# A four-layer graph network: smaller last chunks and two groups' sums a turn in layers 2 and 3, one tile of lanes, gather lists kept or loaded early

## The chip, the cores and the metric

The kernel runs on one core of a Trainium2 chip. A core has five engines with an instruction queue each: PE (matmuls; its weight loads are shown apart, as PEld), DVE (elementwise work, reductions and scans), ACT (activation functions and scaled copies), POOL (here mostly the indirect DMAs, which gather or scatter rows by a list of indices) and SP (plain DMAs). An engine works through its queue in order and waits on semaphores for the others. The metric is the device time of one execution in microseconds; times of ten executions and one profiled execution are given.

## The reference

Four layers act on 6250 nodes with 128 features and 200,000 edges, sorted by their target `dst`. Each layer adds to `x`, from `h = relu(layernorm(x))`. What matters here are layers 2 and 3, both of which weigh edges by a softmax:

```python
# layer 2 (h and edge_weight1 in)
xl = x @ Wl + bl;  xr = x @ Wr + br
m = leaky_relu(xl[src] + xr[dst] + edge_attr @ We, 0.2)
logits = m @ att
ex = exp(logits - segment_max(logits, dst)[dst])
alpha = ex / (segment_sum(ex, dst)[dst] + 1e-16)
out = segment_sum(xl[src] * alpha[:, None], dst)
# x + out, gelu, and a normalisation over the nodes follow

# layer 3 (heads = src, rels = edge_type, tails = dst)
score = sum(e_t * tanh(e_h + e_r), axis=-1)
score_exp = exp(score - max(score))
attn = score_exp / (segment_sum(score_exp, heads)[heads] + 1e-10)
agg = segment_sum(attn[:, None] * e_t, heads)
out = leaky_relu((entity_emb + agg) @ W.T, 0.2)
```

Layer 0 sums `h[src]` over `dst`, layer 1 sums messages made of `(x @ W_in)[dst]` and an edge filter over `src`; dense layers follow in both.

## The kernel before

**Groups.** The edges are cut into 391 groups (`NG`) of 512 (`FE`), that is four tiles (`FT`) of 128 edges, one edge to a partition. A group's targets lie in a window of 64 nodes (`FW`), which begins at a register value (`starts`), so that sums over edges become matmuls against a one-hot matrix. Such a matrix comes from a comparison of `lane`, a tile that holds 0 to 63 in each of four tiles, with `loc`, the edges' targets less the window's start. If the edges are not sorted, or a window is too wide, a general path runs; with these inputs it does not.

**Stages.** Layer 0 gathers rows of `h` by `src` and adds up windows (with the edges' ranks by `src` for layer 1 beside it); layer 1 first makes messages and scatters them in the order of `src` (`messages1`), then reads them back in that order and sums them (`windows1`); `node2` makes the tables `l_tab` and `r_tab`. Layer 2 is `windows2` with `sums2`; `node3` finishes it (`finish2`), and makes `g_tab` and `w_tab`. Layer 3 is `windows3` with `sums3`, and `finish3` writes the output.

**A group in layers 2 and 3** goes through these steps, of which `in_chunks` calls one for one group in each turn:

- `fetch`: four gathers into `m` (POOL, L328, rows of `l_tab` by `src`, or of `g_tab` by `dst`), the window `win` and rows of edge data (SP), and the one-hot matrix `hotT` on DVE (L1196, L1509).
- `near`: four matmuls `pz` (L1204, L1518); in layer 3 a tanh to `z` on ACT (L1520).
- `scores`: DVE makes one score for each edge (L1210 to L1213; L1526).
- `weights`, once for a chunk of 12 groups (`CG`): a running maximum and exponentials in several steps, one step a turn (five `yield`s in layer 2, L1220 to L1279, two in layer 3, L1534 to L1555); its result `ex` goes to `todo`.
- `weighted`: the one-hot `hot` by a comparison with `lane` (DVE, L1291, L1566), times `ex` on ACT (L1293, L1568).
- `sums`: matmuls of `m` by `hot` into `ps` (L1300 and L1301; L1577, and L1578 with a DVE reduction L1574 ahead of it).
- `add`: DVE adds `ps` to `acc` (L1308 and L1311; L1586 and L1587).

A turn fetches group g, weighs one group of `todo`, sums the one weighed a turn ago, does `near` for group g-1 and `scores` for g-2, adds what was summed a turn ago, and takes one step of `weights`. When the last group is fetched, turns go on until `todo` is empty.

**What sets the order.** Except for layer 1's messages, whose order is written out, the framework that builds the program orders each engine's instructions itself: it takes the order of the code as priority and what it reckons to be ready. Buffers come from pools of fixed size: 25 `m` in layer 2 and 27 in layer 3, two `ps`, three `hot`; an instruction that writes a buffer waits for the last reader of the one before.

**Lists.** Layer 0 loads `src` into a tile `src0` in its own pool, which ends with layer 0; layer 2 loads it again (L1162) and layer 3 loads `dst`, in the order of `src`, from `o_tab[1]` (L1475), where layer 1 left it. Layers 0, 1, 2 and 3 each make `lane` with an iota on POOL (L870, L1050, L1168, L1481).

Of the kernel before, what the change touches and what calls it, by code (L numbers as in the profile page):

```python
# [9 lines left out]
F32 = mybir.dt.float32  # L10
I32 = mybir.dt.int32
# [12 lines left out]
P = 128  # L24
# [44 lines left out]
def gnn_kernel(ctx: ExitStack, tc: tile.TileContext, t, out):  # L69
# [108 lines left out]
    bad_b = const.tile([1, 1], I32, name="bad_b")  # L178
    nc.vector.memset(bad_b, 1)

    upto1 = ExitStack()
    pos = upto1.enter_context(tc.tile_pool(name="pos", bufs=1)).tile([P, NG * FT], I32, name="pos")
    upto0 = ExitStack()
    src0 = upto0.enter_context(tc.tile_pool(name="src0", bufs=1)).tile([P, NG * FT], I32, name="src0")
    with tc.tile_pool(name="h", bufs=1) as hp, tc.tile_pool(name="ln", bufs=1) as lp:
        h = hp.tile([P, J, D], F32, name="h")
        norm_relu(lp, h, lambda c: nc.scalar.dma_start(nodes(h_tab)[:, c:c + CJ, :], h[:, c:c + CJ, :]))


        nc.sync.dma_start(first, t["dst_first"].rearrange("(o g) -> o g", o=1))  # L190
        with tc.tile_pool(name="ok", bufs=1) as op, tc.tile_pool(name="ok_ps", bufs=1, space=PSUM) as pp:
            ds_ = op.tile([P, 2, EP // P], I32, name="ds")
            for k in range(2):
                nc.sync.dma_start(ds_[:, k, :], t["dst_pad"][k:k + EP].rearrange("(p n) -> p n", p=P))
            df = op.tile([P, 2, EP // P], F32, name="df")
# [12 lines left out]
            nc.vector.tensor_tensor(fl[:, 1, :], fl[:, 1, :], fl[:, 0, :], op=ALU.subtract)  # L208
            nc.vector.tensor_scalar(fl[:, 1, :], fl[:, 1, :], float(FW) - 0.5, None, op0=ALU.is_gt)
            wide_ = op.tile([1, 1], F32, name="wide_")  # L210
            nc.vector.tensor_reduce(wide_, fl[:, 1, :], axis=AX.X, op=ALU.add)
            pv = pp.tile([1, 1], F32, name="pv")
            nc.tensor.matmul(pv, viol, ones[:, 0:1], start=True, stop=True)
            nc.vector.tensor_tensor(bad, pv, wide_, op=ALU.add)
        nc.sync.dma_start(src0, t["src_f"])


    def load(name, shape, src):
# [631 lines left out]
    def windows0():  # L850

        with ExitStack() as st:
# [3 lines left out]
            with ExitStack() as st:  # L856
# [6 lines left out]
                src = src0  # L863
                rank = ranks(st, src)
                loc = lp.tile([P, NG, FT], F32, name="loc")
                nodes_ = loc.bitcast(I32)
                nc.sync.dma_start(nodes_.rearrange("p g j -> p (g j)"), t["dst_f"])
                nc.vector.tensor_tensor(loc, nodes_, bcast(base, FT), op=ALU.subtract)
                lane = lp.tile([P, FT, FW], F32, name="lane")
                nc.gpsimd.iota(lane, pattern=[[0, FT], [1, FW]], base=0, channel_multiplier=0,  # L870
                               allow_small_or_imprecise_dtypes=True)
# [28 lines left out]
    upto0.close()  # L900


    def messages1():
# [133 lines left out]
    def windows1():  # L1037

        messages1()
        with ExitStack() as st:  # L1040
# [3 lines left out]
            with ExitStack() as st:  # L1044
# [4 lines left out]
                lane = one.tile([P, FT, FW], F32, name="lane")  # L1049
                nc.gpsimd.iota(lane, pattern=[[0, FT], [1, FW]], base=0, channel_multiplier=0,  # L1050
                               allow_small_or_imprecise_dtypes=True)
# [40 lines left out]
        windows1()  # L1092
    with cond.Else():
        zeroed(sums[1])
        phase(edges1, ["f_src", "dst", "w_col", "attr"],
              functions="natural_log_exp_and_others")
        node2(lambda: finish_sums(sums[1], None, w_o1, b_o1, shifted_softplus, w_o2, b_o2))
# [4 lines left out]
    def in_chunks(sp, fetch, near, scores, weights, weighted, sums, add):  # L1102

        sc, ms, todo = None, [], []
        one, two, held = None, None, None
        hot, part = None, None
        g = 0  # L1110
        while g < NG or one or two or held or todo or hot or part:
            new = (g, fetch(g)) if g < NG else None
            new_hot = None
            if todo:
                a, m, i, ex, scale, more = todo.pop(0)
                new_hot = a, weighted(a, m, ex[:, i * FT:(i + 1) * FT], *more), scale
            new_part = (hot[0], sums(hot[0], hot[1]), hot[2]) if hot else None
            new_two = (one[0], near(*one)) if one else None
            if two:
                b, got = two  # L1120
                i = b % CG
                if i == 0:
                    sc, ms = sp.tile([P, CG * FT], F32, name="sc"), []
                ms.append((b, scores(b, got, sc[:, i * FT:(i + 1) * FT])))
            if part:
                add(*part)
            if held:
                try:
                    next(held[0])
                except StopIteration as e:  # L1130
                    ex, scale, *more = e.value
                    todo += [(a, m, a % CG, ex, scale if i == 0 else None, more)
                             for i, (a, m) in enumerate(held[1])]
                    held = None
            if two and (b % CG == CG - 1 or b == NG - 1):
                held = weights(b // CG * CG, len(ms) * FT, sc), ms
                next(held[0])
            one, two, hot, part = new, new_two, new_hot, new_part
            g += 1

    def windows2():
# [9 lines left out]
    def sums2(st, acc):  # L1151
# [6 lines left out]
        pp = st.enter_context(tc.tile_pool(name="ep", bufs=2, space=PSUM))  # L1158
        cp = st.enter_context(tc.tile_pool(name="ec", bufs=2, space=PSUM))
        RW = 2  # L1160
        src = lp.tile([P, NG * FT], I32, name="src")
        nc.sync.dma_start(src, t["src_f"])  # L1162
        loc = lp.tile([P, NG, FT], F32, name="loc")
        nodes_ = loc.bitcast(I32)
        nc.sync.dma_start(nodes_.rearrange("p g j -> p (g j)"), t["dst_f"])
        nc.vector.tensor_tensor(loc, nodes_, bcast(base, FT), op=ALU.subtract)
        lane = lp.tile([P, FT, FW], F32, name="lane")
        nc.gpsimd.iota(lane, pattern=[[0, FT], [1, FW]], base=0, channel_multiplier=0,  # L1168
                       allow_small_or_imprecise_dtypes=True)
# [145 lines left out]
    def node3(finish):  # L1315

        with tc.tile_pool(name="h3", bufs=1) as hp, tc.tile_pool(name="y", bufs=2) as yp, \
                tc.tile_pool(name="y_ps", bufs=2, space=PSUM) as pp, tc.tile_pool(name="ln", bufs=1) as lp:
            finish()
            h = hp.tile([P, J, D], F32, name="h")  # L1320
            rest = hp.tile([FW, D], F32, name="rest")
# [142 lines left out]
    def sums3(st, acc, top):  # L1464
# [15 lines left out]
        lane = lp.tile([P, FT, FW], F32, name="lane")  # L1480
        nc.gpsimd.iota(lane, pattern=[[0, FT], [1, FW]], base=0, channel_multiplier=0,  # L1481
                       allow_small_or_imprecise_dtypes=True)
# [248 lines left out]
```

## Time and profile before

| | us |
|---|---|
| median of ten executions (lowest to highest) | 10489.92 (10475.3 to 10502.91) |
| the profiled execution | 10494.47 |
| its span, first to last instruction | 10492.7 |
| layer 0 | 0 to 2430 |
| layer 1, messages, then sums and `node2` | 2430 to 4950, to 5434 |
| layer 2, then `node3` | 5434 to 7916, to 8028 |
| layer 3, then `finish3` | 8028 to 10447, to the end |
| last gather of layer 2, of layer 3 begins | 7842.84, 10382.1 |

The page gives, over the whole span, PE 6903.5 us busy (66%), DVE 5307.3 (51%), ACT 2292.4 (22%) and POOL 6380.4 (61%). Its second part cuts the span into 40 slices of 262 us; a digit is the busy share in tenths, and PEclk is the clock that was granted to PE, in tenths of full speed. A group of instructions is shown by line, engine and operation, `out<-in`, with its count, then the busy time and the mean in ns, then the idle time ahead of it and what ended it. "issue" is time in which an engine waited for nothing that the profile shows, "remote" or "another core or an unknown queue" a releaser that the profile cannot name. The four-pass float32 matmuls appear as two entries each, so the four matmuls of `near` are "x8". In the instructions in order of time, a line has start, duration, engine, line, operation, and in brackets the idle time before it with its releaser.

### The profile page before, as it was taken

The numbers are of one execution on the slowest core, as the hardware profiler recorded it, in microseconds if no ns is written. First come the engines' busy times: TensorE is split into PE (matmuls) and PEld (weight loads), VectorE is DVE, ScalarE is ACT, GpSimd is POOL, SyncE is SP. The second block draws the span as 40 slices with busy tenths as digits, with TensorE's granted clock in tenths as the row PEclk, the third lists the DMA queues.
The fourth block names the chain that finished last, engine by engine and source line by source line (L and its number), as shares of the span: only waits on it lengthen the run. The fifth ranks groups of instructions, "written<-read, shape, count | busy, mean of one in ns | idle before, by whom it ended". The sixth has DMA issues, their size and how long they took to land.

```text
span 10492.7 us, 122048 instructions
## 1 busy us (share of the span) xinstructions
PE 6903.5 (66%) x31854; PEld 5216.2 (50%) x31854; DVE 5307.3 (51%) x21299; ACT 2292.4 (22%) x6433; POOL 6380.4 (61%) x6281
## 2 busy tenths in 40 slices
PE   4788888855555655555955666666663567777677
PEld 3444444434444444444944454554452466666666
DVE  5455555524444444444765566665664444444445
ACT  0000000003444444443221111111112222222223
POOL 6666666664666666665026777777762566666663
PEclk9755555557777777777986666666665555555555
DMA  2111111113333333333942222222222333333332
GB/s 81 45 47 46 43 43 45 42 46 90 96 98 97 98 97 98 98 98 106 291 150 66 71 72 72 71 73 71 72 65 86 90 96 92 95 93 95 94 94 85
DMA packets 462742, 893.64 MB, mean 85 GB/s; under 512 B 150146, under 2 KB 232501, under 8 KB 461891
## 3 DMA queue, kind: packets, MB, share of 16 engines
q1 hardware_dynamic: 251274, 451.64, 15.1%
q0 software_dynamic: 200192, 412.80, 14.9%
q10 hardware_dynamic: 10556, 21.01, 0.6%
q8 instruction: 281, 4.60, 0.2%
q14 instruction: 439, 3.60, 0.1%
HBM read 750.87 MB, written 133.98 MB: 84 GB/s over the span
## 4 chain that ended last, share of the span: by engine, by line
PE 47%; another core or an unknown queue 21%; DVE 13%; issue 10%; POOL 4%; ACT 3%; DMA 2%; DVEq 0%; SPq 0%; ACTq 0%; POOLq 0%
PE pz L1518 6%; PE ps L1577 5%; PE ps L881 5%; PE pw L973 4%; PE ps L1066 3%; POOL m L328 3%; PE py L975 3%; PE pf L952 3%; PE pq L797 3%; PE ps L1300 3%; PE pz L1204 3%; PE sizes L765 2%; PE pq L798 2%; PE ps L1301 1%
## 5 line engine op out<-in xcount | busy, mean ns | idle before, releaser
L328 POOL DMA_INDIRECT m<-l_tab,src x1564 | 1746.5, 1117 | 662.4 <-issue 409.1
L332 POOL DMA_INDIRECT m_tab<-m,pos x1564 | 1588.2, 1015 | 871.7 <-issue 442.0
L328 POOL DMA_INDIRECT m<-h_tab,src x1564 | 1533.3, 980 | 852.5 <-issue 423.5
L328 POOL DMA_INDIRECT m<-g_tab,dst x1564 | 1506.4, 963 | 847.9 <-issue 411.1
L1518 PE MATMUL pz<-win,hotT 128*128 128x128 f32 x3128 | 848.2, 424 | 360.6 <-issue 282.2
L1577 PE MATMUL ps<-hot,m 128*128 128x64 f32 x3128 | 734.8, 408 | 404.8 <-ACT hot L1568 242.7
L973 PEld LDWEIGHTS pw<-L_gnn_W_f,sp_r 128*128 128x128 f32 x3128 | 496.1, 234 | 960.2 <-issue 918.0
L973 PE MATMUL pw<-L_gnn_W_f,sp_r 128*128 128x128 f32 x3128 | 532.2, 324 | 649.7 <-DVE sp_r L999 463.2
L1577 PEld LDWEIGHTS ps<-hot,m 128*128 128x128 f32 x3128 | 670.1, 313 | 531.2 <-ACT hot L1568 341.8
L1204 PE MATMUL pz<-win,hotT 128*128 128x128 f32 x3128 | 660.6, 369 | 365.8 <-issue 210.6
L1518 PEld LDWEIGHTS pz<-win,hotT 128*128 128x128 f32 x3128 | 712.4, 315 | 371.2 <-issue 316.5
L881 PEld LDWEIGHTS ps<-hot,m 128*128 128x128 f32 x3128 | 731.0, 326 | 299.6 <-issue 111.9
L1204 PEld LDWEIGHTS pz<-win,hotT 128*128 128x128 f32 x3128 | 556.2, 263 | 594.5 <-issue 367.3
L881 PE MATMUL ps<-hot,m 128*128 128x64 f32 x3128 | 722.8, 408 | 192.7 <-DVE acc L883 64.9
L1293 ACT ACTIVATE hot<-hot,ex 128x64 f32<-128x64 f32 x1564 | 415.9, 336 | 1868.1 <-DVE hot L1291 1019.7
L1300 PE MATMUL ps<-hot,m 128*128 128x64 f32 x3128 | 585.0, 347 | 270.5 <-issue 91.2
L983 DVE TENSOR_TENSOR m<-pw,L_gnn_b_f_b 128x512 f32<-128x512 f32 x391 | 267.6, 685 | 961.5 <-remote 660.6
L1300 PEld LDWEIGHTS ps<-hot,m 128*128 128x128 f32 x3128 | 546.7, 262 | 318.9 <-issue 259.9
L975 PE MATMUL py<-win,hotT 128*128 128x128 f32 x3128 | 533.7, 314 | 210.3 <-issue 210.1
L952 PE MATMUL pf<-row_a,w_f1p 128*128 128x512 f32 x782 | 511.2, 728 | 158.6 <-issue 136.1
L1520 ACT ACTIVATE z<-pz 128x512 f32<-128x512 f32 x391 | 232.7, 596 | 1664.2 <-PE pz L1518 887.4
L883 DVE TENSOR_TENSOR acc<-acc,ps 128x64 f32 x391 | 86.7, 222 | 1005.7 <-PE ps L881 456.3
(322 smaller groups left out, 12250.4 us busy)
## 6 DMA issues: line engine op xcount, KB each, us to landing
m<-m_tab SPq DMA_DIRECT2D x391, 262.0 KB
row<-in_dst_row SPq DMA_DIRECT2D x390, 256.0 KB
row<-e_tab SPq DMA_DIRECT2D x390, 256.0 KB
row_w<-in_w_row SPq DMA_DIRECT2D x195, 256.0 KB
m<-h_tab,src POOLq DMA_INDIRECT x1564
m_tab<-m,pos POOLq DMA_INDIRECT x1564
m<-l_tab,src POOLq DMA_INDIRECT x1564
m<-g_tab,dst POOLq DMA_INDIRECT x1564
```

The lines of the kernel that those rows point to most:

```text
L328: nc.gpsimd.indirect_dma_start(out=dst, out_offset=None, in_=table[:], in_offset=bass.IndirectOffsetOnAxis(ap=idx, axis=0))
L332: nc.gpsimd.indirect_dma_start(out=table[:], out_offset=bass.IndirectOffsetOnAxis(ap=idx, axis=0), in_=src, in_offset=None, **kw)
L797: nc.tensor.matmul(pq, pick[:, i:i + 1].to_broadcast([3 * RB, P]), pieces[b], start=True, stop=False)
L881: nc.tensor.matmul(ps, m[:, j, :], hot[:, j, :], start=(j == 0), stop=(j == FT - 1))
L952: nc.tensor.matmul(pf, w_f1p, attrs[g // RW % 3][:, along(g)], start=True, stop=True)
L973: nc.tensor.matmul(pw[:, j, :], sp[:, j * P:(j + 1) * P], w_f2, start=True, stop=True)
L975: nc.tensor.matmul(py[:, j, :], hots[g % 4][:, j * P:(j + 1) * P], wins[g % 8], start=True, stop=True)
L1204: nc.tensor.matmul(pz[:, j, :], hot[:, j * P:(j + 1) * P], win[g % 4], start=True, stop=True)
L1293: nc.scalar.activation(hot[:, j, :], hot[:, j, :], AF.Copy, scale=ex[:, j:j + 1])
L1300: nc.tensor.matmul(ps[:, 0, :], m[:, j, :], hot[:, j, :], start=(j == 0), stop=(j == FT - 1))
L1518: nc.tensor.matmul(pz[:, j, :], hot[:, j * P:(j + 1) * P], win[g % 4], start=True, stop=True)
L1577: nc.tensor.matmul(ps[:, 0, :], m[:, j, :], hot[:, j, :], start=(j == 0), stop=(j == FT - 1))
```

## The change

`lane` and a list `taken` become tiles that live for the whole kernel. `lane` is made once, at the start. `taken` holds `src` from layer 0 through layer 2, so that layer 2 loads nothing; `node3` then loads `o_tab[1]` into it ahead of its own finish, and layer 3 gathers by it. (The general path of layer 1 stores `taken` to `o_tab[1]`; it does not run here.)

In `in_chunks`, chunks end at 12, 24, up to 360, then at 367, 373, 379, 385 and 391: one of seven groups and four of six, in place of two of 12 and one of seven. In turns after the 367th, two groups of `todo` are weighted, and with that summed and added, if two are there. The steps of a turn also come in another order: fetch, add, sums, weighted, near, scores, weights, where before it was fetch, weighted, sums, near, scores, add, weights. All groups are still computed as before.

```diff
+    lane = const.tile([P, FT, FW], F32, name="lane")
+    nc.gpsimd.iota(lane, pattern=[[0, FT], [1, FW]], base=0, channel_multiplier=0,
+                   allow_small_or_imprecise_dtypes=True)
+    taken = const.tile([P, NG * FT], I32, name="taken")
...
-    src0 = upto0.enter_context(tc.tile_pool(name="src0", bufs=1)).tile([P, NG * FT], I32, name="src0")
...
-        nc.sync.dma_start(src0, t["src_f"])
+        nc.sync.dma_start(taken, t["src_f"])
...
+        full = (NG // CG - 2) * CG
+        ends = set(range(CG, full + 1, CG)) | set(range(NG, full + CG // 2 - 1, -(CG // 2)))
+        tail = NG - 2 * CG
         sc, ms, todo = None, [], []
         one, two, held = None, None, None
-        hot, part = None, None
+        hot, part = [], []
         g = 0
         while g < NG or one or two or held or todo or hot or part:
             new = (g, fetch(g)) if g < NG else None
-            new_hot = None
-            if todo:
+            for p in part:
+                add(*p)
+            part = [(a, sums(a, got), scale) for a, got, scale in hot]
+            hot = []
+            for _ in range(2 if g > tail and len(todo) > 1 else min(1, len(todo))):
                 a, m, i, ex, scale, more = todo.pop(0)
-                new_hot = a, weighted(a, m, ex[:, i * FT:(i + 1) * FT], *more), scale
-            new_part = (hot[0], sums(hot[0], hot[1]), hot[2]) if hot else None
+                hot.append((a, weighted(a, m, ex[:, i * FT:(i + 1) * FT], *more), scale))
             new_two = (one[0], near(*one)) if one else None
             if two:
                 b, got = two
-                i = b % CG
-                if i == 0:
-                    sc, ms = sp.tile([P, CG * FT], F32, name="sc"), []
+                if not ms:
+                    sc = sp.tile([P, CG * FT], F32, name="sc")
+                i = len(ms)
                 ms.append((b, scores(b, got, sc[:, i * FT:(i + 1) * FT])))
-            if part:
-                add(*part)
...
-            if two and (b % CG == CG - 1 or b == NG - 1):
-                held = weights(b // CG * CG, len(ms) * FT, sc), ms
+            if two and b + 1 in ends:
+                assert held is None
+                held = weights(ms[0][0], len(ms) * FT, sc), ms
+                ms = []
                 next(held[0])
...
     def sums2(st, acc):
-        src = lp.tile([P, NG * FT], I32, name="src")
-        nc.sync.dma_start(src, t["src_f"])
+        src = taken
-        lane = lp.tile([P, FT, FW], F32, name="lane")
-        nc.gpsimd.iota(lane, ...)
...
     def node3(finish):
+            nc.sync.dma_start(taken, o_tab[1])
             finish()
...
     def sums3(st, acc, top):
-        dst = lp.tile([P, NG * FT], I32, name="dst")
-        nc.sync.dma_start(dst, o_tab[1])
+        dst = taken
-        lane = lp.tile([P, FT, FW], F32, name="lane")
-        nc.gpsimd.iota(lane, ...)
```

More of the change, by code (lines that the diff above doesn't have):

```diff
@@ L179, in gnn_kernel @@
     nc.vector.memset(bad_b, 1)
+    lane = const.tile([P, FT, FW], F32, name="lane")
+    nc.gpsimd.iota(lane, pattern=[[0, FT], [1, FW]], base=0, channel_multiplier=0,
+                   allow_small_or_imprecise_dtypes=True)
+    taken = const.tile([P, NG * FT], I32, name="taken")
     upto1 = ExitStack()
     pos = upto1.enter_context(tc.tile_pool(name="pos", bufs=1)).tile([P, NG * FT], I32, name="pos")
-    upto0 = ExitStack()
-    src0 = upto0.enter_context(tc.tile_pool(name="src0", bufs=1)).tile([P, NG * FT], I32, name="src0")
     with tc.tile_pool(name="h", bufs=1) as hp, tc.tile_pool(name="ln", bufs=1) as lp:
@@ L862, in windows0 @@
                 tp = st.enter_context(tc.tile_pool(name="et", bufs=1, space=PSUM))
-                src = src0
+                src = taken
                 rank = ranks(st, src)
@@ L868, in windows0 @@
                 nc.vector.tensor_tensor(loc, nodes_, bcast(base, FT), op=ALU.subtract)
-                lane = lp.tile([P, FT, FW], F32, name="lane")
-                nc.gpsimd.iota(lane, pattern=[[0, FT], [1, FW]], base=0, channel_multiplier=0,
-                               allow_small_or_imprecise_dtypes=True)
                 own = own_terms(acc, hp, tp)
@@ L898, in gnn_kernel @@
         node1(lambda: finish_sums(sums[0], h_tab, w1_0, b1_0, relu_bias, w2_0, b2_0))
-    upto0.close()
     def messages1():
@@ L1048, in windows1 @@
                 tp = st.enter_context(tc.tile_pool(name="et", bufs=2, space=PSUM))
-                lane = one.tile([P, FT, FW], F32, name="lane")
-                nc.gpsimd.iota(lane, pattern=[[0, FT], [1, FW]], base=0, channel_multiplier=0,
-                               allow_small_or_imprecise_dtypes=True)
                 ids = one.tile([P, NG, FT, IDS], F32, name="ids")
@@ L1094, in gnn_kernel @@
         zeroed(sums[1])
+        nc.sync.dma_start(o_tab[1], taken)
         phase(edges1, ["f_src", "dst", "w_col", "attr"],
@@ L1131, in in_chunks @@
                     ex, scale, *more = e.value
-                    todo += [(a, m, a % CG, ex, scale if i == 0 else None, more)
+                    todo += [(a, m, i, ex, scale if i == 0 else None, more)
                              for i, (a, m) in enumerate(held[1])]
                     held = None
-            if two and (b % CG == CG - 1 or b == NG - 1):
-                held = weights(b // CG * CG, len(ms) * FT, sc), ms
+            if two and b + 1 in ends:
+                assert held is None
+                held = weights(ms[0][0], len(ms) * FT, sc), ms
+                ms = []
                 next(held[0])
-            one, two, hot, part = new, new_two, new_hot, new_part
+            one, two = new, new_two
             g += 1
@@ L1160, in sums2 @@
         RW = 2
-        src = lp.tile([P, NG * FT], I32, name="src")
-        nc.sync.dma_start(src, t["src_f"])
+        src = taken
         loc = lp.tile([P, NG, FT], F32, name="loc")
@@ L1166, in sums2 @@
         nc.vector.tensor_tensor(loc, nodes_, bcast(base, FT), op=ALU.subtract)
-        lane = lp.tile([P, FT, FW], F32, name="lane")
-        nc.gpsimd.iota(lane, pattern=[[0, FT], [1, FW]], base=0, channel_multiplier=0,
-                       allow_small_or_imprecise_dtypes=True)
         node = lp.tile([FW, NG], F32, name="node")
@@ L1479, in sums3 @@
         nc.vector.tensor_tensor(loc, si.rearrange("p (g j) -> p g j", j=FT), bcast(base_b, FT), op=ALU.subtract)
-        lane = lp.tile([P, FT, FW], F32, name="lane")
-        nc.gpsimd.iota(lane, pattern=[[0, FT], [1, FW]], base=0, channel_multiplier=0,
-                       allow_small_or_imprecise_dtypes=True)
         node = lp.tile([P, NG], F32, name="node")
```

## The prediction

> **What bounds the kernel now.** I read the page first, then the chain that ended last, then busy time by stretch, and last the instructions in order of time at the places that the diff touches. The page shows that layers 2 and 3 (slices 21 to 40) are neither idle nor full on any engine, so a share over the whole span decides nothing:
>
> ```profile
> POOL 6666666664666666665026777777762566666663
> PEclk9755555557777777777986666666665555555555
> ...
> L328 POOL DMA_INDIRECT m<-l_tab,src x1564 | 1746.5, 1117 | 662.4 <-issue 409.1
> ```
>
> The stretches tell it better (columns: length, then busy us and count of PE, PEld, DVE, ACT, POOL, then granted PE clock, DMA share, GB/s):
>
> ```profile
> 5650.00:7700.00 2050.00, 1332.48 (x6582) 1009.91 (x6581) 1280.38 (x5793) 370.66 (x1418) 1512.45 (x1346) 0.66 0.27 72
> ...
> 7700.00:7842.00 142.00, 85.90 (x410) 63.56 (x409) 78.21 (x350) 22.64 (x86) 102.84 (x95) 0.64 0.26 69
> 7864.90:7915.90 51.00, 50.40 (x188) 32.99 (x186) 21.68 (x97) 17.91 (x69) 0.00 (x0) 0.50 0.02 3
> 10240.00:10382.00 142.00, 102.55 (x436) 92.91 (x437) 68.19 (x325) 36.88 (x124) 90.71 (x95) 0.52 0.35 95
> 10412.40:10447.20 34.80, 33.44 (x156) 32.60 (x156) 22.74 (x76) 15.30 (x59) 0.00 (x0) 0.52 0.01 1
> ```
>
> Row 1: in layer 2's body POOL is busy 1512 of 2050 us, and POOL's waits there hold 347.5 us of "issue" (0.30 before every gather), together 91%: **the gathers set the pace**, 6.1 us a turn (391 groups of four gathers from 5450 to 7843), and PE idles 35%. Rows 3 and 5: once the last gather and the last score are done, PE alone works, 50.40 of 51.00 us and 33.44 of 34.80 us. These are the **drains**. The chain shows one, a group's sums after another at 1.90 + 0.94 = 2.84 us:
>
> ```profile
> 7906.78 1.90 PE ps L1300 x8
> 7908.68 0.94 PE ps L1301 x2
> 7909.62 1.90 PE ps L1300 x8
> 7911.52 0.94 PE ps L1301 x2
> 7912.46 1.91 PE ps L1300 x8
> 7914.39 3.67 DMA hs<-k_tab
> ```
>
> Row 4: in layer 3 PE is busy 102.55 of 142 us with gathers still running; POOL waits for PE there (146.5 us for pz L1518, 84.0 for ps L1578 from 8250 to 10240), so layer 3 is paced by PE and its round trip over ACT.
>
> The starts of both layers, POOL's instructions in order of time:
>
> ```profile
> 5434.54 0.35 POOL L1168 IOTA lane<- 128x256 f32 x1 [484.04 <-DMA r_tab<-r]
> 5439.37 0.98 POOL L328 DMA_INDIRECT m<-l_tab,src  x1 [4.49 <-DMA src<-in_src_f]
> ...
> 8028.36 0.35 POOL L1481 IOTA lane<- 128x256 f32 x1 [184.58 <-DMA w_tab<-w]
> 8033.39 0.97 POOL L328 DMA_INDIRECT m<-g_tab,dst  x1 [4.68 <-DMA dst<-o_tab]
> ```
>
> At 5434.54 POOL may run, but the first gather waits until 5439.37 for the list `src`; likewise at 8028.36 for `dst`.
>
> **The change part by part.** The working is made against the profiled execution: 10494.47 us, a span of 10492.7 and 1.77 around it; it lies 4.55 above the median of the ten, 10489.92.
>
> *Lists kept (layer 2) or loaded early (layer 3).* Layer 2's load goes, layer 3's is issued in `node3` ahead of its finish. SP has nothing from the last gather (7842.84) to 7910.72 but that, the same load took some 5 us at 8028.20, and the first that queues behind it is a small store that nobody awaits; cost 0. Without that cover it would push back the `d_tab` store of 7916.04 by 5 us. The first gather moves to where POOL was free (the iota, 0.35 us, goes too): 5439.37 - 5434.54 = 4.8 and 8033.39 - 8028.36 = 5.0. From there to 5590 and to 8179 the chain is mostly waits on an unseen queue in steps of about 22 us per four groups, which is the gathers' landing, so an earlier first gather should move all of it. What is late next is DVE's memsets and loads (first compare at 5453.31 and 8052.22), but those feed the first groups only. I take -4.8 and -5.0. Bounds: 0 each if DVE's preparation gates; +3.3 for layer 2, since one early gather took 8.16 us (at 5441.92, under DVE's 10.62 us memset), and a second of that length would cost 8.16 - 4.8.
>
> *Lanes in one tile.* Four iotas of 0.35 us become one. Those of layers 0 and 1 (34.9, 4937.9) stand before a first compare at 53.9 and 4955.2: 0. Those of layers 2 and 3 lie inside the list's wait, counted above.
>
> *Chunks and two sums a turn.* Writing both loops out turn by turn: 412 turns become 403 in layer 2 and 409 become 400 in layer 3; sums left after the last score fall from 18 to 12 and from 15 to 6; 8 groups' sums move ahead of the last fetch in layer 2, and 9 ahead of the last score in layer 3. Each layer has two chunks more (35 for 33).
>
> Layer 2 drain: six sums fewer, 6 x 2.84 = 17.0. New on the path: the last chunk's weights. In the trace they take 7865.56 to 7878.57, 13.0 us; six other sums (17.0) now lie beside them, so they are hidden, but the first `hot` after them is not: 0.41 on DVE and 0.35 on ACT, about 1. Drain -16. Without that cover it would be -17 + 13. The turns 390 to 392, the last with a score, have no sums, so the 22.1 us from the last gather to the last score shrink: -2 (0 to -5). POOL's five long waits between 7690 and 7845 (3.82, 1.38, 2.75, 1.82, 2.11) are for `m` buffers; live groups fall from 21 of 25 to 12 to 16, so they can go: a third, -4 (0 to -11.9). What pays is 8 x 2.84 = 22.7 us of PE inside 142 - 85.9 = 56 us of PE idle. Taken: **-22**. Bounds: -33 with every wait gone; +6.7 if the moved sums lengthen the turns by all they cost (22.7 - 16).
>
> Layer 3 drain: nine sums fewer at 1.71 + 0.43 = 2.14 are 19.2; the weights (max, matmul, max, matmul, exp) now stand alone with about 4. So -15. But here PE paces the turns: the nine cost 9 x (1.97 + 0.53) = 22.5 us of 39.5 us idle, of which about 1.0 a turn (pz ends, ACT's z 0.60, first `hot` 0.35, then sums) comes once in each of 23 turns however many sums it has. 39.5 - 23 = 16.5 is open, 6 is paid. Taken: **-9**; bounds -15 and +7.5 (22.5 - 15).
>
> The added chunks: layer 2's weights are some 5.4 us on DVE and 2.4 on PE, twice, beside gathers: 0, or +11 without them.
>
> *`add` first in the turn.* The `add` of the turn before now stands ahead of sums, weighted and scores. It frees a `ps` buffer (there are two) earlier. The row for it:
>
> ```profile
> PE ps L1300 <- DVE acc L1311: 69.8, 66, 3.0
> ```
>
> 69.8 us is the most that can be had, and PE is not the bound there: POOL leaves 9% open, 69.8 x 0.09 = 6. Taken -6, bounds -69.8 and 0 for layer 2, since 0.81 us of `add` (0.40 + 0.20 + 0.21) ahead of `hot` fits into PE's 2.4 idle us a turn. In layer 3 the order already stands so in time (acc at 10366.01, hotT 10366.22, hot 10367.09): 0.
>
> On the clock: the drain of layer 2 is 99% busy and was granted 0.50; between 7857 and 7863 the same sums took 1.08 + 0.59 = 1.67 us at a higher clock. The Trainium skill (TensorE: Matmul & The Clock Gate, Part 1: The HAM clock gate) says that half rate is the default and that about 3.4 us of sustained activity releases it. By that the six sums would be worth 6 x 1.67 = 10 instead of 17. The row speaks against it for these matmuls, and the row is used above.
>
> Sum: -4.8 - 5.0 - 22 - 9 + 0 - 6 = **-46.8**: 10447.7 for the profiled execution, 10443.1 when it is taken from the median, as all times below are.
>
> **Rivals.** *The work is hidden nowhere:* moved sums lengthen the turns by their full price. For it: layer 3's PE pace, the ACT round trip. Against: PE's 56 us idle in layer 2. -9.8 + 6.7 + 7.5 = +4.4: 10494. (That the lists bring nothing, since DVE gates, adds 9.8 to any case.)
>
> *The new order pays in full:* PE's 69.8 us all come back. For it: the long chain of DVE work behind which `add` stood. Against: POOL's 91%. -46.8 - 63.8 = -110.6: 10379.
>
> *Slower, by the order in layer 3:* `both` (L1574) waits for ACT's `hot` 113 times, 123.3 us in all; it now stands ahead of the `hot` compare L1566 on DVE. Should each wait pass on to L1566, ACT and PE's sums, layer 3 pays 123.3: -46.8 + 123.3 = +76.5, 10566. It decides from 46.8 + 21 = 67.8 us on, over half of these waits. Against: L1566 at 10367.09 is consumed only a turn later.
>
> **How the numbers follow.** 0.2% (21 us) is about what a measurement of this kernel tells from no change. Forecast 0.55, its own range -25 to -65 (starts by half, -5, with layer 2's drain of -16 and layer 3's at -4; or -9.8 - 33 - 15 - 6, all bounds of gain but the order's): 10425 to 10465. Hidden nowhere 0.17, the "same" case. New order 0.15. Slower 0.13. Faster is 0.55 + 0.15 = 0.70. The range reaches from the new order's 10379, rounded to 10380, to 10500, past the hidden case; what it leaves out is the slower case and a little at the low end.
>
> **What would show it.** Right: the first gathers of layers 2 and 3 directly behind the landing of `r_tab` and `w_tab`; 12 and 6 groups' sums after the last score; the drains about 35 and 20 us long; the body of each layer as long as before to within 10 us. Wrong: turns of 8 us from group 368 on in layer 3; POOL waiting for `m` in the tail; a body of layer 2 or 3 changed by more than 20 us, which only the order can do. If DVE gates the starts, the first scores stand where they stood.

## The result, and the profile after

The changed kernel takes **10525.33 us** (median; 10514.13 to 10534.62) against 10489.92: the ratio is 1.0035, with a 95% interval of 1.0026 to 1.0043. It is slower, where 10443 was forecast and faster was given 0.70. Its profiled execution took 10505.74 us (span 10503.9), some 20 us less than its median, so its trace holds only 11 of the 35 us.

From the page of the changed kernel, the lines that answer to those of before:

```profile
POOL 6666666664666666665025767777753566666663
PEclk9655555557777777777976666666655655555556
...
L331 POOL DMA_INDIRECT m<-l_tab,taken x1564 | 1664.2, 1064 | 1208.8 <-issue 887.6
```

Layer 2's gathers became shorter (1064 ns each for 1117), and POOL waits longer instead. Its first gathers, in order of time:

```profile
5417.51 0.98 POOL L331 DMA_INDIRECT m<-l_tab,taken  x1 [482.87 <-issue]
...
8027.39 0.94 POOL L331 DMA_INDIRECT m<-g_tab,taken  x1 [219.78 <-issue]
```

Layer 2's first gather starts 21.9 us earlier, not 4.8: with iota and list gone, it doesn't wait for `r_tab` either. Last the tails, as busy time by stretch with the prediction's columns; first of the kernel before, from the 341st group's score to the last score of layer 2, and from there to the last `add`; then the same two stretches of the changed kernel, and its two of layer 3:

```profile
7572.90:7862.22 289.32, 197.67 (x963) 148.38 (x962) 186.79 (x847) 54.25 (x209) 200.84 (x180) 0.66 0.26 69
7862.22:7915.68 53.46, 51.97 (x196) 34.29 (x196) 24.14 (x111) 18.68 (x72) 0.00 (x0) 0.52 0.02 2
```

```profile
7542.01:7877.06 335.05, 242.47 (x1049) 183.57 (x1049) 202.18 (x924) 62.17 (x241) 185.59 (x177) 0.58 0.23 61
7877.06:7914.93 37.87, 35.35 (x134) 22.89 (x134) 16.41 (x79) 11.63 (x46) 0.00 (x0) 0.50 0.02 2
10150.48:10439.60 289.12, 200.53 (x995) 183.94 (x993) 151.00 (x728) 90.80 (x303) 154.92 (x161) 0.59 0.31 83
10439.60:10460.15 20.55, 17.99 (x81) 16.91 (x80) 11.36 (x45) 6.57 (x27) 0.00 (x0) 0.50 0.00 0
```

The drain is 15.6 us shorter, but the stretch ahead of it 45.7 us longer: layer 2's tail, which was to give 22 us, costs 30. The whole ledger follows, from the instructions in order of time. Marks: a, the first gather of the layer; b, c, d, the scores of groups 25, 341 and 391; e, the last `add`. The right-hand columns are for the experiments below (`before_again`, `after_third` and `fix_pool`).

| us | before | changed | quick chip: before | changed | list on POOL |
|---|---|---|---|---|---|
| a of layer 2 stands at | 5439.4 | 5417.5 | 4665.7 | 4654.9 | 4647.7 |
| layer 2, a to b | 208.2 | 220.1 | 143.8 | 144.3 | 143.7 |
| b to c, the body | 1925.3 | 1904.4 | 1817.6 | 1700.1 | 1698.4 |
| c to d | 289.3 | 335.0 | 286.0 | 327.5 | 276.5 |
| d to e, the drain | 53.5 | 37.9 | 54.0 | 37.9 | 37.9 |
| e to layer 3's a | 117.7 | 112.5 | 115.3 | 113.5 | 112.7 |
| layer 3, a to b | 218.8 | 226.2 | 126.3 | 126.6 | 126.6 |
| b to c | 1888.6 | 1896.9 | 1625.4 | 1600.9 | 1601.8 |
| c to d | 271.0 | 289.1 | 256.1 | 252.8 | 252.4 |
| d to e | 35.1 | 20.5 | 38.8 | 22.7 | 22.7 |

Left half: -21.9 + 11.9 - 20.9 + 45.7 - 15.6 - 5.2 + 7.4 + 8.3 + 18.1 - 14.6, and -2.0 behind it, are the 11 us.

### The profile page after: what moved, and what is told of

It reads as the page before. It is cut to its first block, busy times and chain, and to the rows that moved or that the text cites. A ratio compares the mean times of both kernels' runs of the same rounds, so it can differ in the third digit from the quotient of the medians.

```text
span 10503.9 us, 122031 instructions
## 1 busy us (share of the span) xinstructions
PE 6937.9 (66%) x31894; PEld 5247.7 (50%) x31894; DVE 5296.7 (50%) x21363; ACT 2315.0 (22%) x6443; POOL 6296.5 (60%) x6278
## 3 DMA queue, kind: packets, MB, share of 16 engines
q1 hardware_dynamic: 251162, 450.84, 15.2%
## 5 line engine op out<-in xcount | busy, mean ns | idle before, releaser
L331 POOL DMA_INDIRECT m<-l_tab,taken x1564 | 1664.2, 1064 | 1208.8 <-issue 887.6
L331 POOL DMA_INDIRECT m<-g_tab,taken x1564 | 1506.3, 963 | 1074.5 <-issue 622.7
L331 POOL DMA_INDIRECT m<-h_tab,taken x1564 | 1533.7, 981 | 874.0 <-issue 421.2
L1201 PE MATMUL pz<-win,hotT 128*128 128x128 f32 x3128 | 770.0, 392 | 456.2 <-issue 208.6
L1512 PE MATMUL pz<-win,hotT 128*128 128x128 f32 x3128 | 845.5, 423 | 203.7 <-issue 144.0
L1201 PEld LDWEIGHTS pz<-win,hotT 128*128 128x128 f32 x3128 | 611.5, 276 | 696.2 <-issue 396.3
L1571 PE MATMUL ps<-hot,m 128*128 128x64 f32 x3128 | 724.6, 401 | 350.6 <-ACT hot L1562 219.1
L1571 PEld LDWEIGHTS ps<-hot,m 128*128 128x128 f32 x3128 | 677.7, 312 | 404.5 <-ACT hot L1562 231.7
L881 PEld LDWEIGHTS ps<-hot,m 128*128 128x128 f32 x3128 | 722.4, 323 | 304.1 <-issue 117.8
L881 PE MATMUL ps<-hot,m 128*128 128x64 f32 x3128 | 713.6, 405 | 190.6 <-DVE acc L883 69.0
L1512 PEld LDWEIGHTS pz<-win,hotT 128*128 128x128 f32 x3128 | 700.7, 311 | 223.9 <-issue 188.5
L1297 PE MATMUL ps<-hot,m 128*128 128x64 f32 x3128 | 641.3, 359 | 257.0 <-ACT hot L1290 179.3
L1297 PEld LDWEIGHTS ps<-hot,m 128*128 128x128 f32 x3128 | 609.7, 278 | 311.3 <-ACT hot L1290 210.4
L956 ACT ACTIVATE sp_a<-pf,L_gnn_b_f_c 128x512 f32<-128x512 f32 x391 | 267.9, 685 | 1415.7 <-remote 923.1
```

Of the source, the lines that this page charges most:

```text
L331: nc.gpsimd.indirect_dma_start(out=dst, out_offset=None, in_=table[:], in_offset=bass.IndirectOffsetOnAxis(ap=idx, axis=0))
L881: nc.tensor.matmul(ps, m[:, j, :], hot[:, j, :], start=(j == 0), stop=(j == FT - 1))
L956: nc.scalar.activation(a, pf, AF.Abs, bias=b_f1)
L1201: nc.tensor.matmul(pz[:, j, :], hot[:, j * P:(j + 1) * P], win[g % 4], start=True, stop=True)
L1297: nc.tensor.matmul(ps[:, 0, :], m[:, j, :], hot[:, j, :], start=(j == 0), stop=(j == FT - 1))
L1512: nc.tensor.matmul(pz[:, j, :], hot[:, j * P:(j + 1) * P], win[g % 4], start=True, stop=True)
```

## The experiments

**Two kinds of chip.** The runs fell on chips of two kinds. On two of them the kernel before took 10490 and 10387 us ("slow kind"; the first measurement is from one), on six others 9177 to 9195 us ("quick kind"). The difference is there in layer 0, which no edit touches in substance: its gathers take 2382 us on the first chip and 2008 on a quick one. No chip was measured at two times, so the runs don't tell whether a kind belongs to the chip or to the time. Instructions in order of time on the slow kind (kernel before), PE's and then DVE's:

```profile
1010.32 1.81 PE L881 MATMUL ps<-hot,m 128*128 128x64 f32 x8
```

```profile
1014.85 0.22 DVE L883 TENSOR_TENSOR acc<-acc,ps 128x64 f32 x1 [4.87 <-remote]
```

and POOL's next gather, whose buffer PE's sums must have read:

```profile
1015.08 0.98 POOL L328 DMA_INDIRECT m<-h_tab,src  x1 [2.64 <-remote]
```

PE's sums end at 1012.13 by the record; the `add` that needs them starts at 1014.85, and nothing that the profile names holds it. From 600 to 2000 us such a lag of over 1 us stands in 71 of 228 groups (199 us in all; 75 and 70 in the changed kernel's two traces from there), often 17.4 us apart; in `before_again`, on a quick chip, in 2 of 277. (The expectations below give 72 of 235 and 3 of 285, a first count that took some groups twice.) DVE's waits without a named releaser ("remote") come to 2222 us in the whole trace of the kernel before on the first chip; in `before_again`, `after_third` and `order`, on quick chips, there are none. The granted clock is 0.5 or 1 on both kinds. So PE seems to stop there, unseen: two engines that need its sums go on at nearly the same moment. This is inferred from what waits for PE; no record shows a stop. The Trainium skill (Perfetto Trace Analysis, Per-engine timelines) says that the profiler estimates the end of a matmul instead of observing it; these lags agree, since a stop behind the record would look like this.

Theories at the start: **P**, two sums a turn cost the tail; **W**, the half chunks do; **O**, the new order does. Later: **B**, only half chunks and pairs together do it; **C**, the chip decides; **H**, unseen stops of PE make what waits for PE dear; **S**, layer 3's list load holds SP.

| kernel | kind | ratio to before, 95% |
|---|---|---|
| changed | slow | 1.0035 (1.0026 to 1.0043) |
| after_again: changed | slow | 1.0049 (1.0036 to 1.0063) |
| order_again | slow | 1.0021 (1.0012 to 1.0030) |
| tail | slow | 1.0035 (1.0021 to 1.0048) |
| after_third: changed | quick | 0.9836 (0.9822 to 0.9850) |
| lists, lists_again | quick | 0.9998 and 1.0005 (0.9989 to 1.0014) |
| lists_fix | quick | 0.9996 (0.9987 to 1.0005) |
| order | quick | 0.9815 (0.9802 to 0.9829) |
| two, two_again | quick | 0.9815 and 0.9817 (0.9800 to 0.9830) |
| chunks, chunks_again | quick | 0.9826 and 0.9827 (0.9812 to 0.9841) |
| ord2 | quick | 0.9851 (0.9836 to 0.9866) |
| best | quick | 0.9791 (0.9778 to 0.9805) |
| fix_pool, _2, _3 | quick | 0.9778, 0.9787, 0.9783 (0.9765 to 0.9802) |

**Parts of the change, on a quick chip.** `lists` has the `in_chunks` of before. `order` undoes both hunks below in the changed kernel, `two` only the first, `chunks` only the second.

```diff
-        ends = set(range(CG, full + 1, CG)) | set(range(NG, full + CG // 2 - 1, -(CG // 2)))
+        ends = set(range(CG, NG, CG)) | {NG}
...
-            for _ in range(2 if g > tail and len(todo) > 1 else min(1, len(todo))):
+            for _ in range(min(1, len(todo))):
```

> Only lists and lanes of the change; the loop over chunks is that of before (12 groups to a chunk, one sum a turn, add last). In the changed kernel the first gather of layer 2 stood 21.9 us earlier than before and that of layer 3 6.0 us earlier. Theory P (two sums a turn cost the tail their price and more), theory W (the short chunks' weights cost it) and theory O (the new order of the turn costs it) agree here: the starts' gain is kept, 20 to 28 us under the kernel before, 10462 to 10470. If the early starts are themselves lost in the body (waits for m, or a rate set elsewhere), it is within 10 us of before.

> Lists and lanes and the new order of a turn (add, sums, weighted, near, scores), with the old chunks of 12 and one sum a turn. P and W: the tails are as before, layer 2's body gives a further 14 us and layer 3's body takes 12 us more, as in the trace of the changed kernel; with the starts about 25 to 30 us under before, 10460 to 10465. O: the order itself delays the scores in the tail, so layer 2 loses its 35 us here already and the time is at or above before, 10490 to 10525.

> As the changed kernel, but one group's sums a turn throughout: half-size last chunks and the new order stay. P: the 35 us that layer 2's tail lost come back, since the pairs are gone; 10455 to 10475. W: the loss stays, since five short chunks put a step of weights, with its round trips between PE and DVE, into every turn; 10500 to 10525.

> As the changed kernel, but with the old chunks of 12 and a last one of 7: two groups' sums a turn from turn 368 on and the new order stay. P: the loss stays, 10500 to 10530. W: the loss is gone, 10445 to 10475.

The expectations were for a chip like the first. Here the order alone brings 1.85%, which neither P, W nor O had; `two` adds nothing to it, `chunks` loses 0.1%; the lists bring nothing. So neither half of the tail's edit alone costs more than about 0.1%.

**The changed kernel and two of its parts, on a slow chip.** `tail` keeps lists, half chunks and pairs and puts the turn back into the old order:

```diff
-            for p in part:
-                add(*p)
-            part = [(a, sums(a, got), scale) for a, got, scale in hot]
-            hot = []
+            new_hot = []
...
-                hot.append(...)
+                new_hot.append(...)
+            new_part = [(a, sums(a, got), scale) for a, got, scale in hot]
...
+            for p in part:
+                add(*p)
             if held:
...
-            one, two = new, new_two
+            one, two, hot, part = new, new_two, new_hot, new_part
```

> The changed kernel itself, beside the kernel before on one chip. The runs so far came from a chip on which the kernel before takes 9186 us and the gathers of layer 0, which no edit touches, follow at 5.1 us a group; on the chip of the first measurement it was 10490 us and 6.1 us a group. Theory C (the chip decides: where the gathers follow slowly they hide what the new order of the turn gains in layer 2's body): on a chip with 5.1 us a group the changed kernel is 1.6 to 2.0% faster than before (9005 to 9040 us where before is 9186), and on one with 6.1 us a group 0.2 to 0.5% slower again. Against it (the chips alike for this change, and the whole loss in the combination of half chunks with two sums a turn): slower than before by 0.3% on either.

> Lists and lanes, half-size last chunks and two groups' sums a turn, with the old order of a turn (weighted, sums, near, scores, add). Theory C: without the new order nothing is gained in the bodies; on a chip with 5.1 us a group within 0.3% of before, while the changed kernel is 1.6 to 2.0% under it; on one with 6.1 us a group 0.1 to 0.4% over before, since the tail's loss stays. Against it (the tail brings what the prediction gave it, 31 us): 0.3% under before on either chip.

> Lists, lanes and the new order, old chunks, one sum a turn, beside the changed kernel on one chip. On a chip with 5.1 us a group: 1.85% under before as measured there. On one with 6.1 us a group: theory P or W (the pairs or the half chunks lose layer 2's tail) gives 25 to 35 us under before, 0.3%; theory O (the order loses it) gives 0 to 0.4% over before.

All three are slower than before: +25 us with the order, +38 with the tail, +53 with both. So the order costs here, and the tail's edit too. The three traces, from one chip, price each part by an edit:

| us | `tail` | `order_again` | changed (`after_again`) |
|---|---|---|---|
| layer 2, a to c | 2111.9 | 2096.9 | 2102.3 |
| c to d | 324.7 | 284.9 | 327.7 |
| d to e | 37.0 | 53.6 | 37.9 |
| layer 3, a to c | 2084.0 | 2109.0 | 2110.8 |
| c to d | 291.8 | 271.3 | 295.9 |
| d to e | 27.1 | 36.2 | 20.9 |

The order (first column against the last) gives 9.6 us in layer 2 up to c and costs 26.8 in layer 3. The tail's edit (second against last) costs 42.8 us from c to d of layer 2 and gives 15.7 in the drain; in layer 3 it costs 24.6 and gives 15.2. In the medians the order costs 14 us and the tail's edit 28. O had the order delay the scores of layer 2's tail; that is not so, as the 284.9 us with the order alone show. For layer 2, c to d, `order_again` and then `after_again`:

```profile
7488.14:7773.03 284.89, 194.75 (x955) 147.48 (x955) 186.58 (x848) 55.22 (x211) 192.13 (x178) 0.68 0.25 71
```

```profile
7487.04:7814.77 327.73, 224.70 (x1050) 169.97 (x1050) 201.61 (x924) 62.27 (x241) 187.57 (x177) 0.61 0.22 62
```

The last gather begins at nearly the same time after c in both (265.5 and 261.1 us), but behind it 13 groups are still to be scored in the changed kernel, against 6. So it is not the gathers that are late but what follows them.

What the order does here is seen in layer 3's waits from 8300 to 10200 us (engine, line and releaser, then us, times, longest), of before and then of the changed kernel, both from the first chip:

```profile
DVE acc L1586 <- remote: 117.9, 32, 9.4
...
PE ps L1578 <- DVE both L1574: 1.9, 2, 1.5
```

```profile
DVE acc L1580 <- remote: 379.2, 78, 11.0
...
PE ps L1572 <- DVE both L1568: 213.5, 96, 9.2
```

With `add` first in the turn, DVE's unnamed waits ahead of it are three times as long (all its waits ahead of this `add`: 558 and 781 us), and `both`, which stood ahead of `add` and now stands behind it, keeps PE waiting in turn. Much of that takes the place of other waits: PE's waits in this window come to 568 and 583 us in all. The body (b to c) is 8.3 us longer; on quick chips, whose traces have no such lags, it is 24.5 shorter.

**The changed kernel again, and the order in layer 2 alone** (`ord2`: one copy of the loop for each layer, the old order in layer 3, old chunks, one sum a turn); these fell on a quick chip.

> The changed kernel, as the measure for the three runs beside it. Chips of two kinds have shown so far: one on which the kernel before takes 9186 us, and two on which it takes 10390 to 10490 us and on which, in layer 0 already (untouched), DVE starts the add of a group over 1 us after PE's recorded end in 72 of some 235 groups against 3 of 285. Theory H (on the slow kind PE stops for some us at a time, unseen by its records, and whatever is queued behind a wait for PE stops with it): slow kind 0.3 to 0.5% over before, as twice measured; quick kind 1.5 to 1.9% under before, since there the new order pays in layer 2. If the tail's loss is not of the slow kind alone, it is 25 to 35 us over the kernel with the new order alone on the quick kind too (9040 to 9050 where before is 9186).

> Lists and lanes, old chunks, one sum a turn; the new order of a turn in layer 2 alone, the old order in layer 3. Theory H: on the slow kind layer 3's body gets back what the add ahead of everything on DVE cost there (the wait of add for a releaser that the profile can't name went from 118 to 447 us in 1900 us), 15 to 30 us under the kernel with the new order in both layers, so 0 to 30 us under before (-0.3 to 0%). On the quick kind layer 2 keeps its 150 us and layer 3 loses its 30 us: 1.4 to 1.6% under before. Against H: within 5 us of the kernel with the new order in both layers (0.2% over before on the slow kind).

> As the changed kernel but with the old chunks of 12. Theory P (the pairs cost the tail): slow kind as the changed kernel, 0.4 to 0.5% over before. Theory W (the half chunks cost it): 0.2% over before, as the new order alone. Theory B (only both together move sums ahead of the last score, and these sums cost more there than they save): 0.1 to 0.25% over before. On the quick kind 1.85% under before, as measured there.

> As the changed kernel but with one group's sums a turn. P: slow kind 0.2% over before, as the new order alone. W: 0.4 to 0.5% over before. B: 0.2 to 0.3% over before, the added weights alone. On the quick kind 1.74% under before, as measured there.

`ord2` stands 31 us over `two_again` on the same chip, so the order pays some 30 us in layer 3 on the quick kind, where it costs on the slow. On the quick kind the changed kernel is 1.64% faster, but short of its own order alone: half chunks and pairs together lose what neither does alone. Its trace names the place. SP's queue and DVE (`after_third`), then its busy time in a stretch there:

```profile
6702.29 0.47 SPq L1185 DMA_DIRECT2D win<-r_tab  x1
6764.22 0.36 SPq L1316 DMA_DIRECT2D taken<-o_tab  x1
6764.69 0.50 SPq L1190 DMA_DIRECT2D row<-in_dst_row  x1
```

```profile
6770.01 0.48 DVE L1193 TENSOR_SCALAR hotT<-row,node 64x512 f32<-64x512 int32 x1 [51.72 <-DMA row<-in_dst_row]
```

```profile
6720.00:6760.00 40.00, 0.00 (x0) 0.00 (x0) 0.00 (x0) 0.00 (x0) 30.25 (x33) 0.50 0.18 53
```

`taken<-o_tab`, layer 3's list, overwrites the list that layer 2 still gathers by, so it waits for the last gather (6760.56). In the built program SP has it ahead of 8 window, 5 row, 4 weight-row and 2 `d` loads of layer 2; with `two` ahead of 3, 2 and 1 (window, row, weight row), with `order`, `chunks` and `lists` of one window and one row load. For 51.7 us only POOL works. That is S. On the slow kind, in the changed kernel, the same wait is short, since SP comes to it only 4 us before the last gather begins:

```profile
SPq L1316 <- DMA m<-l_tab,taken: 7.7, 1, 7.7
```

**The list behind the gathers.** `fix_pool` changes one line of the changed kernel; `lists_fix` does so in `lists`; `best` has it too, with the tail's edit in layer 3 alone.

```diff
-            nc.sync.dma_start(taken, o_tab[1])
+            nc.gpsimd.dma_start(taken, o_tab[1])
             finish()
```

> The changed kernel with one line changed: layer 3's list is loaded from POOL's queue, behind the gathers that read the tile, in place of SP's, where 8 window and 5 row loads of layer 2 stood behind it. Theory S (that load holds SP, and SP the tail of layer 2): quick kind, the idle 50 us of layer 2's tail go and its drain keeps the 16 us gained, so 35 to 55 us under the changed kernel, 2.0 to 2.3% under before. Slow kind: 8 to 15 us under the changed kernel, 0.3 to 0.4% over before, if PE's unseen stops are the rest (theory H); back to 0 to 0.1% over before if S is all of it. Against S: as the changed kernel within 10 us on either kind.

> Lists and lanes with the list's load on POOL's queue; layer 2 with the new order, old chunks and one sum a turn (NOT the half chunks), layer 3 with all of the change... except that here layer 2 keeps the old order of a turn too. Quick kind: without the new order in layer 2 its 150 us are not gained; layer 3 gives some 30 us by the order and 17 by its shorter drain: 0.4 to 0.6% under before. Slow kind: layer 2 as before, layer 3 about 8 us longer in its body, 20 in its tail and 14 shorter in its drain: 0.1 to 0.3% over before.

> Lists and lanes alone, the loop over chunks as before. Quick kind: as measured there, within 0.1% of before. Slow kind: theory H gives 5 to 20 us under before (the first scores of both layers come earlier, and nothing else changes); if the list's load or the early gathers cost there, 0.1 to 0.3% over before.

> The kernel before, for its trace on the chip of these runs. On the slow kind every theory expects DVE's add of layer 0 to start over 1 us after PE's recorded end in some 70 of 235 groups, on the quick kind in 3 of 285; gathers of layer 0 at 6.1 and at 5.1 us a group.

(The `best` that ran has the new order in both layers; its expectation speaks of another kernel for layer 2, so its numbers don't apply.) `after_third` from c to d, then `fix_pool` from c to d and d to e:

```profile
6499.29:6826.83 327.54, 224.51 (x1034) 169.90 (x1034) 203.10 (x924) 61.38 (x237) 202.18 (x198) 0.63 0.23 66
```

```profile
6489.73:6766.25 276.52, 231.53 (x1037) 174.65 (x1037) 202.76 (x923) 61.35 (x237) 206.56 (x199) 0.62 0.27 78
6766.25:6804.14 37.89, 35.38 (x135) 22.90 (x134) 16.38 (x79) 11.64 (x46) 0.00 (x0) 0.50 0.01 2
```

The stretch falls by 51 us, from 327.5 to 276.5, with the same 57 sums in it, and the drain stays short. 0.9836 becomes 0.9778: **S holds on the quick kind**, and this version beats both kernels there. `best`, on the same chip, lacks only the tail's edit in layer 2: its stretch from c to d is 270.6 us with 50 sums, its drain 53.6. So with SP free the edit gives 9.8 us in the traces and 15.7 in the medians (8990.07 and 8974.38; the intervals overlap), where 22 were forecast. `fix_pool` was measured twice more, for the slow kind, and fell on quick chips:

> The changed kernel with the list's load on POOL's queue, again. Slow kind (before at 10390 to 10490 us): 0.3 to 0.4% over before if PE's unseen stops are most of the loss there (theory H), 0 to 0.1% over or under before if the load on SP is all of it (theory S). Quick kind (before at 9180 us): 2.0 to 2.3% under before, as measured.

> The changed kernel with the list's load on POOL's queue, a third time. Slow kind (before at 10390 to 10490 us): 0.3 to 0.4% over before if PE's unseen stops are most of the loss there (theory H), 0 to 0.1% over or under before if the load on SP is all of it (theory S). Quick kind (before at 9180 us): 2.0 to 2.3% under before, as twice measured.

> Lists and lanes alone, loop over chunks as before, and the load of layer 3's list on POOL's queue behind layer 2's gathers. Theory S (the hold on SP eats the starts' gain): 10 to 25 us under before on either kind, since the 18.7 us for which DVE waited for a row load go and the earlier starts stay. Against it (the starts bring nothing, since what feeds the first groups is late anyway): within 8 us of before, as with the load on SP.

`lists_fix` is within 8 us of before (-4): the hold was not what ate the starts' gain, and no gain of the starts is seen in the time.

**What the order pays on the quick kind.** Waits in layer 2 from 4900 to 6500 us and the gathers' group (`before_again`), then the group in `order`:

```profile
DVE z L1210 <- DMA m<-l_tab,src: 511.7, 229, 5.4
...
PE ps L1300 <- DVE acc L1311: 308.2, 140, 5.6
```

```profile
L328 POOL DMA_INDIRECT m<-l_tab,src x1564 | 1767.3, 1130 | 480.8 <-issue 321.9
```

```profile
L331 POOL DMA_INDIRECT m<-l_tab,taken x1564 | 1636.1, 1046 | 960.8 <-issue 859.0
```

DVE's `z` waits for the newest gather to land, and `add` stood behind `z`, so PE's sums waited for `ps`: 308 us in 1600, where the slow chip had 69.8 in the whole layer. With `add` first this wait is no longer among those listed. But PE's wait is not what the body's length goes by: from b to c every gap between two gathers is 0.30 us in both traces, so POOL sets the pace, 4 x (1.13 + 0.30) = 5.7 us a turn before and 4 x (1.05 + 0.30) = 5.4 in `order`. Each gather takes 0.084 us less, 131 us in 1564, and that is the gain. On the first chip the gathers became shorter too (1117 to 1064 ns), but there POOL's waits of over 0.4 us grew from 139 to 210 us from b to c, about what the gathers gave. Why they are shorter was not tried. The Trainium skill (SBUF — State Buffer, SBUF: two separate sides) says that some DVE operations lock POOL out of ports that both use, and so keep it from writing the descriptors of its DMAs. Which operation would do it here, no run shows.

## Why the prediction was wrong, by its own steps

On the chip of the forecast the terms and their outcomes in the trace, in its order: starts, -9.8 forecast and -7.8 measured (up to group 25 of each layer); layer 2's tail, -22 and +30.1; layer 3's tail, -9 and +3.5; the order in the bodies (b to c), -6 and -12.6; behind layer 3, -2.0. So the tails failed, layer 2's above all. On the quick kind the term that failed is another, the list's load.

- **Layer 2's tail, -22**: this is the step that failed on the first chip. The drain fell by 15.6 (-16 was said), with 12 sums left, as said; the error is the overlap, that the moved sums hide in "56 us of PE idle". From c to d the stretch grew by 45.7 us for 7 sums (20 us at 2.84 each) and two more weights, with PE's busy time up by 44.8 and its granted clock down from 0.66 to 0.58; on the second slow chip the edit alone cost 42.8 there. The idle time was read from records that don't show when PE is stopped, if the lags are stops of PE. On the quick kind, with SP free, the moved sums do hide for the most part: 276.5 us for 57 sums against 270.6 for 50.
- **Lists, cost 0** ("SP has nothing from the last gather ... but that"): I took the load to stand where the code has it. The program put it ahead of up to 19 loads that layer 2 still needed, and one tile for both lists made it wait for layer 2's gathers. Price on the quick kind 51 us in the trace (327.5 to 276.5), 0.5 to 0.6% in time. On the slow kind the wait is 7.7 to 9.5 us, and it can have made the loads behind it no later than that.
- **Starts, -4.8 and -5.0**: the gathers did start earlier (-21.9, -6.0), but by group 25 the gain is 10.0 us in layer 2 and in layer 3 it is gone, and `lists` and `lists_fix` show no gain (-4 us, -12 to +5). A bound of 0 had been given, "if DVE's preparation gates". In layer 3 the first score came at 8053.55, 2.0 us earlier, not 6.0, which fits that bound; in layer 2 it came 18.3 us earlier, and what took the rest was not isolated. That the two terms together come near the forecast is luck.
- **Layer 3's tail, -9**: the drain gave 14.6 and 16.1. The moved sums cost 18.1 on the first chip and 24.6 on the second slow one (22.5 was their full price, 6 what I took) and nothing on the quick.
- **`add` first, -6 and 0**: on the first chip -20.9 in layer 2's body against +15.7 in layer 3 (a to c), on the second -9.6 and +26.8; in time, `order_again` with its lists stands 25 us over before on the slow kind. On the quick kind -117 in layer 2's body and -24.5 in layer 3's, most of the 1.6 to 1.9%. "POOL leaves 9% open" took the gathers' own duration as fixed; it is not.
- **Rivals**: the likeliest case lost to a mixture. "Hidden nowhere" is what the slow kind shows of the moved sums, and more than their price in layer 2. "Slower, by the order in layer 3" named the right layer and the right instruction, `both`, but the wrong path and price: not a wait passed on to L1566, 123 us, but PE waiting for `both` behind an `add` that waits for PE. The order's price in layer 3 was 16 and 27 us; that this path makes all of it was not tried.

**Open**: on the slow kind no run of `fix_pool`, `ord2`, `two`, `chunks` or `lists` fell. There S is bounded by SP's wait, 7.7 of the 45.7 us and 8.5 of the 42.8, but which half of the tail's edit costs the rest, and what the lists do, was not measured. That PE's stops make the rest of the tail's loss is argued from the lags, the waits and the clock, not shown.

## What to carry to other kernels

When an edit loads early into a tile that is still being read, look up where the load stands in its queue and what stands behind it; if the readers run on one engine, issue the load from that engine's queue, behind them. An idle share is free room only if the engine could have run: check recorded ends against the start of what waits for them. One chip's profile prices one chip: the order of a turn was worth 1.8% on one kind and less than nothing on the other.

## What the runs showed of the hardware

The same program on one core took 9186 us on one chip and 10490 on another, 14% more, in layer 0 as in the others (2008 and 2382 us of gathers). With it go lags behind PE's recorded ends (71 of 228 groups, 199 us in 1400, on a quick chip 2 of 277), which the granted clock does not show. And a gather's instruction is not of fixed length: 1.13 us in one order of DVE's work, 1.05 in another, on one kind of chip, and that set the pace of a layer.
